# Attention scores and mixes made beside the second aggregation pass by TensorE products, with a scattered tail for sources of the last 14 node tiles

## The chip, the cores and the metric

The kernel runs on one NeuronCore of a Trainium2 chip. A core has five engines with queues of their own: TensorE (PE, with its weight loads shown as PEld), VectorE (DVE), ScalarE (ACT), GpSimd (POOL) and SyncE (SP). SP and ACT issue plain DMAs; POOL issues the indirect DMAs, which gather or scatter rows by indices that lie in on-chip memory (SBUF). PSUM is the small memory that PE writes. The time is the device time of one execution in microseconds (us), as a median of runs.

## The reference, cut to what matters

There are N = 12500 nodes of D = 256 features and 200000 edges sorted by their target `dst`. Two blocks follow each other: a graph convolution in two passes (each a sum over edges into the target node, then a product with a weight), and one attention block.

```python
h = relu(layernorm(x));  x = x + gcn(h)          # two passes over all 200000 edges
h = relu(layernorm(x))
xt = (h @ weight).reshape(n, 4, 64)              # 4 heads of 64
alpha_l = einsum('ehd,hd->eh', xt[src], attn_l)  # per edge, per head
alpha_r = einsum('ehd,hd->eh', xt[dst], attn_r)
alpha = softmax(leaky_relu(alpha_l + alpha_r, 0.01), axis=heads)
tmp = einsum('nh,nhd->nd', alpha[:n], xt[dst[:n]])   # only the FIRST n edges are used
out = x + tile(tmp, 4)
```

The attention block uses only the first n = 12500 edges, one per output row: row e of the output needs the scores of edge e. Since the edges are sorted by target, the targets of these edges are the first few hundred nodes (up to node 788 in the drawn inputs), while their sources lie anywhere among all nodes.

## The kernel before, in words

Nodes are handled in NT = 98 tiles of P = 128. Edges are handled in tiles of 128 too, J = 14 tiles to a chunk, NCH = 112 chunks. After a preparation of some 130 us come two passes over all edges, both made by `convolve` (L1153). For each edge tile, POOL gathers the 128 source rows from a table in DRAM (L1374, tile `fgot`), DVE makes one-hot matrices of the targets for a whole chunk (L1241, tile `fhot`), and PE multiplies the two and sums in PSUM (L1382, tile `facc`). `fgot` has four buffers of one chunk each in pass 2, so POOL can run ahead of PE by up to three whole chunks and the rest of one. A finished chunk is turned (`turn_sums`, L1202 to L1208) and added to a running transposed buffer (L1293). When all edges of a node tile w have been added, its finishing steps are queued.

The order of the work on every engine is written out by hand, in slots: one slot is one edge tile `t`. `at(t, step)` (L1167) puts a step down for a later slot, and `run(t)` (L1392) emits, after each tile's product, the steps that are due. In pass 2 the finishing steps of node tile w come from `finish2` (L1464), at offsets 6 to 28 slots: the products with the last two weights, the residual sum `fx` (stored to `kept_x`, L1495), the layernorm (L1497 to L1509), the transposes (L1514), and the product `fpx` with `fwg` (L1527). `fwg` holds the attention weight and, as eight more columns, that weight folded with `attn_r` and `attn_l`. So `fpx` gives, per node, its row xt, four right scores and four left scores. The left scores go to a DRAM table `table_l` (and to `table_e`, which leaves out the last three tiles), and for the first nine node tiles xt and the right scores go to `table_r`. Near the end of a pass the offsets are shortened to one slot each.

SP's queue holds, per node tile, the loads of the next tile's rows (`rb`, `fxb`, `self`) and the store of `kept_x`. An instruction that waits holds up all that stand behind it on its engine, and DMAs of one issuing engine follow each other.

After the second pass comes the attention's own stage, which we call the tail. The row of an edge's target, xt and right scores, is a product of a one-hot matrix (`hot_t`, L1572) and a gathered block of `table_r` (`rows`, L1577), copied out by ACT (`fends` to `fxg`, L1652 and L1654). For the first chunk this is done in pass 2 already. The left scores of an edge's source are gathered by POOL from `table_l`, one indirect DMA per tile of 128 edges (`fal`, L1662): 98 of them. DVE then adds, takes the softmax over the heads (L1669 to L1678), mixes the heads (L1685 to L1692) and adds the residual (`fres`, L1694), in 13 groups of G = 7 tiles and a last one split in two; SP loads `kept_x` (`fxr`, L1624) and stores the output (L1700, L1703). The first two groups are gathered from `table_e`, and what the last three tiles lack there is added by products (`lacks`, L1633).

Of the kernel before, what the change touches and what calls it, by code (L numbers as in the profile page):

```python
# [8 lines left out]
F32 = mybir.dt.float32  # L9
# [404 lines left out]
def fast_path(  # L414
# [62 lines left out]
    assert AC * J == NT and AC * CE <= E and XW < NT  # L477
    table_r = dram.tile([XW * P, DR], F32, name="table_r")
    table_l = dram.tile([NT * P, H], F32, name="table_l")

    LW = 3
    table_e = dram.tile([NT * P, H], F32, name="table_e")
# [18 lines left out]
    base_b = const.tile([P, NCH], F32, name="base_b")  # L501
    row_i = const.tile([P, AC], I32, name="row_i")
# [88 lines left out]
    with tc.tile_pool(name="fprep", bufs=1) as prep:  # L591
# [233 lines left out]
        with tc.tile_pool(name="fpsum", bufs=2, space=PSUM) as psum, \  # L825
# [227 lines left out]
            wide = prep.tile([NCH, P], F32, name="wide")  # L1053
            nc.vector.tensor_copy(wide, base.to_broadcast([NCH, P]))
# [7 lines left out]
            nc.tensor.matmul(fk[:, 2, :NCH], wide, ident[:NCH, :NCH], start=True, stop=True)  # L1062
# [7 lines left out]
            for f in after:  # L1070
                f()
            after = [raw_block(ends, m, psum.tile([P, 4 * P], F32, name="ft"), j0)
                     for j0 in (8, 12)]
            nc.vector.tensor_copy(base_b, fk[:, 2, :NCH])
            nc.vector.tensor_scalar(row_i, base_b[:, :AC], lane, float(XW * P - 1), op0=ALU.add,
                                    op1=ALU.min)
# [16 lines left out]
    def check_chunks(work, psum):  # L1093
# [20 lines left out]
        kept = work.tile([1, 1], F32, name="n_kept", bufs=1)  # L1114
        nc.vector.tensor_reduce(kept, pt[:1, 2, :NCH], AX.X, ALU.add)
        nc.vector.tensor_add(kept, kept, counted)
        nc.vector.tensor_scalar(bad_row, kept, -1.0, float(NCH + 1), op0=ALU.mult, op1=ALU.add)
# [12 lines left out]
    def load_late(pool):  # L1130

        nc.scalar.dma_start(roots, root_t)
        for t, w in ((wb, w2), (wo, w_post), (wg[:, :, :D], w_gat)):
            nc.scalar.dma_start(t, w.rearrange("(k p) n -> p k n", p=P))
        nc.scalar.dma_start(b2c, b2.rearrange("(k p) -> p k", p=P))
# [8 lines left out]
    def late_weights(pool, attn):  # L1144

        for i, ar in enumerate(attn):
            for k in range(KC):
                prod = pool.tile([P, H, C], F32, name="fprod", bufs=1)
                nc.vector.tensor_mul(prod.rearrange("p h c -> p (h c)"), wg[:, k, :D], ar)
                nc.vector.tensor_reduce(wg[:, k, D + i * H:D + (i + 1) * H], prod, AX.X,  # L1150
                                        ALU.add)

    def convolve(ep, table, stride, width, ahead, with_sum, psum, prepare, finish, lacking=False,  # L1153
                 raw=(), rows_p=None):
# [28 lines left out]
        def run(now=None):  # L1183

            while due:
# [3 lines left out]
                do(d)  # L1189

# [41 lines left out]
        const_p = psum.tile([P, P if with_sum else P + D], F32, name="iota_p", bufs=1)  # L1232
# [520 lines left out]
```

## Time and profile before

| what | value |
|---|---|
| median of 5 runs (lowest to highest) | 4148.24 us (4144.22 to 4149.51) |
| the profiled execution's own time | 4153.36 us |
| its span, first to last instruction | 4151.4 us |
| mean granted TensorE clock | 0.805 of full speed |
| busy: PE, PEld, DVE, ACT, POOL | 3083.6, 1955.9, 1139.4, 491.4, 3104.3 us |
| gathers of the passes (L1374) | 3056 with 947 ns each |
| gathers of the tail (L1662) | 98, 95.3 us busy in all |
| HBM traffic | 498.89 MB read, 53.21 MB written |

How to read it: "busy" counts only executing instructions, and an average over the whole span mixes the preparation, the two passes and the tail, which have different limits. Between two gathers POOL is always idle for 0.30 us with the cause "issue", that is, it waited for nothing that the profile shows; so a gather costs POOL 1.25 us and not 0.95.

### The profile page before, as it was taken

To read this page: it belongs to the slowest core of one execution; us is meant where nothing else is said; L and a number is where in the kernel's file an instruction comes from. 1 tells how busy PE (TensorE), PEld (TensorE's weight loads), DVE (VectorE), ACT (ScalarE), POOL (GpSimd) and SP (SyncE) were. 2 spreads that over 40 slices of the span, in tenths; PEclk is the share of its full clock that TensorE was granted. 3 is DMA by queue.
4 is the path that set the end of the run, shared out by engine and by line. 5 is a ranking of instruction groups with operands and counts; after the bars stand their busy time and mean duration, and the time that the engine had idled before them with its cause. 6 is when DMAs were issued, how large, how long until landed. Compare 5 with 4: busy or idle time off the path is not lost. (4 is left out here: it accounts for less than half of the span.)

```text
span 4151.4 us, 32267 instructions
## 1 busy us (share of the span) xinstructions
PE 3083.6 (74%) x10600; PEld 1955.9 (47%) x10600; DVE 1139.4 (27%) x2421; ACT 491.4 (12%) x1233; POOL 3104.3 (75%) x3299
## 2 busy tenths in 40 slices
PE   6687887877788877877587777776777777777774
PEld 5464444444444444443365545554555544544562
DVE  8532111111111111111232222222222222222238
ACT  5400000000000000000011111111111111111122
POOL 7677777777777777777777777777777777777766
PEclk8698778788877778788698888788878888888877
DMA  8644444444444444444544544554555445554556
GB/s 270 194 126 122 120 120 120 122 120 120 120 122 120 120 120 121 120 119 120 150 125 134 131 128 126 128 131 128 128 128 132 128 128 128 132 127 125 131 158 205
DMA packets 327420, 554.57 MB, mean 134 GB/s; under 512 B 96302, under 2 KB 224837, under 8 KB 327245
## 3 DMA queue, kind: packets, MB, share of 16 engines
q0 software_dynamic: 153520, 414.16, 37.8%
q1 hardware_dynamic: 127878, 121.99, 9.7%
q10 hardware_dynamic: 45846, 16.27, 1.6%
q8 instruction: 87, 1.43, 0.1%
q14 instruction: 89, 0.72, 0.1%
HBM read 498.89 MB, written 53.21 MB: 133 GB/s over the span
## 5 line engine op out<-in xcount | busy, mean ns | idle before, releaser
L1374 POOL DMA_INDIRECT fgot<-ftable,fsrc_t x3056 | 2892.5, 947 | 947.8 <-issue 880.2
L1382 PE MATMUL facc<-fgot,fhot 128*128 128x257 f32 (+1 forms) x6252 | 2335.2, 493 | 901.2 <-DMA fgot<-ftable,fsrc_t 859.5
L1382 PEld LDWEIGHTS facc<-fgot,fhot 128*128 128x128 f32 x6252 | 1252.1, 230 | 1824.4 <-DMA fgot<-ftable,fsrc_t 1402.8
L1293 DVE TENSOR_TENSOR buf<-buf,fturn 128x256 f32 x224 | 94.5, 422 | 1635.5 <-PE fturn L1206 1305.6
L1241 DVE TENSOR_TENSOR fhot<-iota_p,to_t 128x1792 f32<-128x1792 f32 x224 | 448.8, 2004 | 4.4 <-PE fpt L1267 4.4
L1479 DVE SCALAR_TENSOR_TENSOR fy<-rb,fb2c,fpz 128x128 f32<-128x128 f32 x194 | 58.8, 345 | 722.4 <-PE fpz L1472 721.4
L1276 ACT ACTIVATE fsums<-facc 128x257 f32<-128x257 f32 (+1 forms) x224 | 86.2, 385 | 1172.7 <-PE facc L1382 1158.3
L1493 DVE SCALAR_TENSOR_TENSOR fx<-fpo,fdinv,fxb 128x256 f32<-128x256 f32 x97 | 46.9, 484 | 496.1 <-PE fpo L1488 496.1
L1417 PE MATMUL fpo<-wf,buf 128*128 128x256 f32 x388 | 153.8, 540 | 0.3 <-DVE buf L1293 0.3
L1422 ACT ACTIVATE fo<-fpo,fdinv 128x256 f32<-128x256 f32 x97 | 46.0, 474 | 748.3 <-PE fpo L1418 746.5
L1417 PEld LDWEIGHTS fpo<-wf,buf 128*128 128x128 f32 x388 | 111.6, 288 | 28.0 <-DVE buf L1293 0.8
L1472 PE MATMUL fpz<-buf,fwb 128*128 128x128 f32 x776 | 116.5, 299 | 0.0
L1472 PEld LDWEIGHTS fpz<-buf,fwb 128*128 128x128 f32 x776 | 113.3, 221 | 2.1 <-DVE fy L1479 0.3
L1206 PE MATMUL fturn<-fident,self 128*128 128x128 f32 x396 | 83.7, 297 | 37.0 <-DMA to_all<-in_src_dram 24.1
L1488 PE MATMUL fpo<-fwo,fz 128*128 128x256 f32 x388 | 110.8, 410 | 0.1
L1662 POOL DMA_INDIRECT fal<-table_l,fsrc_t x84 | 81.5, 970 | 25.6 <-issue 23.2
L1206 PE MATMUL fturn<-fident,fsums 128*128 128x128 f32 x448 | 95.2, 298 | 0.5 <-ACT fsums L1276 0.5
L1652 PE MATMUL fends<-rows,hot_t 128*128 128x260 f32 x168 | 65.5, 548 | 35.9 <-ACT fxg L1654 35.2
L1518 ACT ACTIVATE ht<-fpt 128x256 f32<-128x256 f32 x97 | 37.2, 384 | 446.3 <-PE fpt L1514 446.3
L668 POOL DMA_INDIRECT fgot<-in_x_dram,raw_i x56 | 74.5, 1331 | 15.4 <-issue 15.1
L1206 PEld LDWEIGHTS fturn<-fident,fsums 128*128 128x128 f32 x448 | 69.7, 156 | 30.9 <-issue 7.6
L1418 PE MATMUL fpo<-bb,fins 2*128 2x256 f32 x194 | 83.0, 513 | 0.0
(267 smaller groups left out, 1720.2 us busy)
## 6 DMA issues: line engine op xcount, KB each, us to landing
fgot<-ftable,fsrc_t POOLq DMA_INDIRECT x3056
self<-ftable SPq DMA_DIRECT2D x99, 128.0 KB
self<-ftable SPq DMA_DIRECT2D x97, 130.0 KB
ftable<-fo ACTq DMA_DIRECT2D x98, 128.0 KB
kept_x<-fx SPq DMA_DIRECT2D x98, 128.0 KB
fxb<-in_x_dram SPq DMA_DIRECT2D x97, 128.0 KB
fxr<-kept_x SPq DMA_DIRECT2D x13, 896.0 KB
out_dram<-fres SPq DMA_DIRECT2D x13, 896.0 KB
```

Of the source, the lines that this page charges most:

```text
L668: nc.gpsimd.indirect_dma_start(out=raw[c][:, j, :D], out_offset=None, in_=x[:], in_offset=bass.IndirectOffsetOnAxis(ap=raw_i[:, k:k + 1], ...
L1206: nc.tensor.transpose(v["pt"][:, i * KC + k, :], rows[:, k * P:(k + 1) * P], ident)
L1241: nc.vector.tensor_tensor(h, iota_p[:, None, :].to_broadcast([P, n, P]), to[:, :, None].to_broadcast([P, n, P]), ALU.is_equal)
L1276: nc.scalar.activation(sb, acc, AF.Copy)
L1293: nc.vector.tensor_add(b, b, v["pt"][:, :KC, :])
L1374: nc.gpsimd.indirect_dma_start(out=got, out_offset=None, in_=table[:(NT - TW) * P, :] if some else table[:], in_offset=bass.IndirectOffset ...
L1382: nc.tensor.matmul(acc, hots[c][:, j, :], got[:, :width], start=(j == 0), stop=(j == nj[c] - 1 and not some))
L1417: nc.tensor.matmul(po, buf[:, k, :P], wf[:, k, :], start=(k == 0), stop=False)
L1418: nc.tensor.matmul(po, fs, bb, start=False, stop=True)
L1472: nc.tensor.matmul(pz[:, m, :], wb[:, k, m * P:(m + 1) * P], buf[:, k, :P], start=(k == 0), stop=(k == KC - 1))
L1488: nc.tensor.matmul(po, v["z"][:, m, :], wo[:, m, :], start=(m == 0), stop=(m == KC - 1))
L1662: nc.gpsimd.indirect_dma_start(out=al[:, i, :], out_offset=None, in_=(table_l if c else table_e)[:], in_offset=bass.IndirectOffsetOnAxis(a ...
```

## The change

The tail of before is taken out. Its work is put in small pieces into the free places of pass 2 (and a list is made in pass 1), and a short new tail treats the edges whose source lies in the last 14 node tiles (84 to 97), of which the drawn inputs have 1707 among the first 12500; the list has room for 2048.

- In pass 1, once 11 node tiles are finished, `list_late` makes, by products with one-hot matrices, a compact list of those "late" edges (KL = 16 columns of 128) with their place, their source and their target; it also stores to DRAM the low seven bits of the sources (`lo_rows`) and the targets relative to the first target of each tile (`rel_rows`).
- `convolve` gets a second queue, `behind`. `feed(t)` takes the next item from it when the item's condition holds and the place is free, and puts its parts into consecutive slots.
- In pass 2 the items are, in this order: load the target rows of each edge tile (98 loads from `table_r` at an address held in a register), the right scores (`alpha_r`, 14 groups of 7 tiles), the one-hots and target rows of the late edges (to DRAM), the left scores in five stages (`alpha_l`, after 18, 36, 54, 72 and 84 node tiles; each stage multiplies a one-hot of the low bits with the left scores of its node tiles, now kept in SBUF as `l_all`, and masks by the high bits), and with the fifth stage the softmax, the mix by products, the residual sum and the store (`group`).
- `table_l`, `table_e`, the 98 gathers of `fal`, the seven gathers of `rows`, the `hot_t`, `hot_l` and `lacks` work are gone.
- After pass 2, for the late edges: 16 gathers of `kept_x`, left scores by 16 products, softmax, mix and 16 indirect scatters of whole rows into the output.

```diff
+    STAGES = [(0, 18), (18, 36), (36, 54), (54, 72), (72, 84)]
+    LATE = STAGES[-1][1]
+    KL = 16
+    LIMITS = [LATE if k < 10 else LATE + G if k == 10 else NT for k in range(KL)]
...
+        def feed(t):
+            if behind and t >= free_at[0] and behind[0][0]():
+                _, space, parts = behind.pop(0)
+                for i, part in enumerate(parts):
+                    if part:
+                        at(t + i, lambda _, part=part: part())
+                free_at[0] = t + space
...
+            feed(t)
             run(t)
-        run()
+        if at_end:
+            at_end()
+        while due or behind:
+            t += 1
+            feed(t)
+            run(t)
...
         def r():
-            if w < NT - LW:
-                xa = work.tile([P, DA], F32, name="fxa")
-            else:
-                xa = lates[w]
-            nc.scalar.activation(xa[:, d0:], v["px"], AF.Copy)
-            nc.scalar.dma_start(table_l[w * P:(w + 1) * P, :], xa[:, DR:])
-            if w < NT - LW:
-                nc.scalar.dma_start(table_e[w * P:(w + 1) * P, :], xa[:, DR:])
             if w < XW:
-                nc.scalar.dma_start(table_r[w * P:(w + 1) * P, :], xa[:, :DR])
+                xa = work.tile([P, DR], F32, name="fxa", bufs=1)
+                nc.scalar.activation(xa, v["px"][:, :DR], AF.Copy)
+                nc.scalar.dma_start(table_r[w * P:(w + 1) * P, :], xa)
+            nc.scalar.activation(l_all[:, w, :], v["px"][:, DR - d0:], AF.Copy)
+            mark("w", w)
...
+        def row_of(rows, b, name, bufs):
+            r = ap.tile([P, HE], BF16, name=name, bufs=bufs)
+            nc.sync.dma_start(r, rows[b * G:(b + 1) * G, :].rearrange("t p -> (t p)")
+                              .partition_broadcast(P))
+            return r
+        def hot_of(row, col):
+            hot = new_hot()
+            nc.vector.scalar_tensor_tensor(hot, row, 0.0, banks[col].to_broadcast([P, HE]),
+                                           op0=ALU.subtract, op1=ALU.is_equal)
+            return hot
+        def ends_of_tile(t):
+            at = start_of(t, (XW * P - NB) * H)
+            nc.sync.dma_start(ends[:, t, :], by_head[bass.ds(at, P), :])
...
+        def alpha_l(s, b):
+            def load():
+                v["row"] = row_of(lo_rows, b, "lo_all", 1)
+            def equal():
+                v["h"] = hot_of(v["row"], "lane")
+            def product():
+                v["p"] = bank()[:, :G * nw * H].rearrange("p (t w h) -> p t w h", t=G, h=H)
+                for j in range(G):
+                    nc.tensor.matmul(v["p"][:, j, :, :], v["h"][:, j * P:(j + 1) * P],
+                                     l_all[:, w0:w1, :], start=True, stop=True)
+            def taken():
+                mask = ap.tile([P, G, 18], F32, name="mask", bufs=1)[:, :, :nw]
+                nc.vector.tensor_tensor(mask, ... ALU.is_equal)
+                nc.vector.tensor_tensor(v["p"], v["p"], ... ALU.mult)
+                nc.vector.tensor_reduce(some, v["p"].rearrange("p t w h -> p t h w"), AX.X, ALU.add)
+                nc.vector.tensor_add(al[:, t, :], al[:, t, :], some)
+            return [load, None, equal, product, taken]
+        def group(b):
+            def load():
+                load_lo()
+                v["rel"] = row_of(rel_rows, b, "rel_all", 2)
+                if whole:
+                    v["kept"] = load_kept(b * G, G)
...
+            return [load, None, equal, product, taken, lambda: v["soft"][0](),
+                    lambda: v["soft"][1](), turn, turned, over(0, 4), weigh(0, 4), over(4, G),
+                    weigh(4, G), mix, end]
...
+        for t in range(0, NT, G):
+            items.append((when("w", XW), G, [lambda t=t + i: ends_of_tile(t) for i in range(G)]))
+        for b in range(NG):
+            items.append((when("w", XW), 4, alpha_r(b)))
+        for b in range(KL // 4):
+            items.append((when("w", XW), 6, late_hots(b)))
+        for k in range(KL):
+            items.append((when("w", XW), 4, late_ends(k)))
+        for s in range(len(STAGES) - 1):
+            for b in range(NG):
+                items.append((when("w", STAGES[s][1]), 4, alpha_l(s, b)))
+        for b in range(NG):
+            items.append((when("w", LATE), 8, group(b)))
+        for t0, n in ((LATE, G), (LATE + G, 4), (LATE + G + 4, 3)):
+            items.append((when("x", t0 + n), 1, rest(t0, n)))
...
+    def tail_begins():
+        rows_x.close()
...
+        nc.sync.dma_start(sets["hot"], late_hot)
+        nc.sync.dma_start(sets["end"], late_end[:].rearrange("(k p) d -> p k d", p=P))
...
+        fetch_x(LATE + G)
...
+        for k in range(KL):
+            nc.tensor.matmul(z[k // 8][:, k % 8, :, :], sets["hot"][:, k * P:(k + 1) * P],
+                             l_all[:, LATE:, :], start=True, stop=True)
...
+        for n in [2, 2] + [4] * ((KL - 4) // 4):
+            nc.vector.tensor_mul(near, heads[:, k, :, :C], ...)
+            nc.vector.tensor_reduce(mix, near.rearrange("p k h c -> p k c h"), AX.X, ALU.add)
+            nc.vector.tensor_tensor(res, res, ... ALU.add)
+            for i in range(k0, k0 + n):
+                nc.gpsimd.indirect_dma_start(
+                    out=out[:], out_offset=bass.IndirectOffsetOnAxis(ap=late_i[:, 0, i:i + 1],
+                                                                     axis=0),
+                    in_=sets["x"][:, i, :], in_offset=None)
```

`load_kept` loads seven tiles of `kept_x` (896 KB) into one of two buffers, and `end` of a whole group adds the mix to it and stores it to the output from the same buffer. `late_ends` and `late_hots` each make 128 (or 4 times 128) one-hots, transpose them, and store their result to DRAM; `rest` adds the mixes of the last 14 tiles to `kept_x` and stores them.

In the order that is built, every scatter into the output waits for the landing of the scatter before it, since all write the same tensor; the loads of `tail_hot` and `tail_end` stand in SP's queue ahead of the last node tile's loads of `rb` and `fxb`; and the load of `lo_all` for group b + 2 stands in SP's queue behind the store of group b's output.

## The prediction

> **What bounds the kernel now.** I read the groups by cost first, then the sums by stretch for pass 2 and the tail, then the timeline at the seams.
>
> ```profile
> span 4151.4 us, 32267 instructions
> ...
> L1374 POOL DMA_INDIRECT fgot<-ftable,fsrc_t x3056 | 2892.5, 947 | 947.8 <-issue 880.2
> L1382 PE MATMUL facc<-fgot,fhot 128*128 128x257 f32 (+1 forms) x6252 | 2335.2, 493 | 901.2 <-DMA fgot<-ftable,fsrc_t 859.5
> ```
>
> POOL waits for nothing ("issue"); PE waits for the gathers. The passes last as long as POOL has gathers to issue, 0.947 + 0.30 = 1.25 us each.
>
> ```profile
> 2026.00:3986.00 1960.00, 1403.36 (x5349) 984.95 (x5348) 526.20 (x1103) 235.32 (x625) 1480.93 (x1564) 0.82 0.50 130
> 3991.00:4151.00 160.00, 89.48 (x300) 60.91 (x300) 113.86 (x223) 39.93 (x116) 97.59 (x101) 0.69 0.63 198
> ```
>
> Columns: stretch, length, busy PE, PEld, DVE, ACT, POOL with counts, granted clock, DMA share, GB/s. In pass 2 PE has 28% free, DVE 73%, the DMA engines half. The tail is 160 us long.
>
> ```profile
> 2026.75 0.94 POOL L1374 DMA_INDIRECT fgot<-ftable,src  x1 [2.15 <-DMA ftable<-fo]
> 2071.62 2.08 PE L1382 MATMUL facc<-fgot,fhot 128*128 128x256 f32 x4 [3.10 <-DVE fhot L1241]
> ...
> 3985.49 0.95 POOL L1374 DMA_INDIRECT fgot<-ftable,fsrc_t  x1 [0.30 <-issue]
> 3989.40 1.46 PE L1382 MATMUL facc<-fgot,fhot 128*128 128x256 f32 x6
> 4005.73 0.94 POOL L1662 DMA_INDIRECT fal<-table_e,fsrc_t  x1 [11.79 <-DMA table_l<-fxl]
> 4129.62 0.94 POOL L1662 DMA_INDIRECT fal<-table_l,fsrc_t  x1 [0.30 <-issue]
> 4144.73 0.70 SPq L1703 DMA_DIRECT2D out_dram<-fres  x1
> ```
>
> At pass 2's start PE begins 45 us after POOL's first gather and POOL never waits: PE may fall 45 us behind unseen. PE's last edge product ends at P = 3990.86. From there to the end are 160.5 us, of which 98 gathers of left scores take 98 x 1.25 = 122 us on POOL. That is what the change removes.
>
> **The change, part by part.**
>
> *POOL in pass 2.* Gone: one gather of `rows` (1.25 us) and the wide integer compares (L1572, L1595) at its start, beside which four gathers took 1.42, 1.46, 1.53 and 1.82 us instead of 0.95, that is 2.4 us. POOL paces, so -3.7 us. The new compares take an operand from PSUM, as `fhot` does, beside which gathers keep 0.95. If all 84 new one-hot operations of 896 columns cost POOL 0.5 us, it would be +42; I take 0, by `fhot`.
>
> *The list in pass 1.* 14 times three wide operations (about 1.0, 0.2 and 0.8 us by the columns of similar DVE rows) and some 60 small ones of 0.2 us are 40 us of DVE in 124 slots (155 us), where DVE is 18% busy, and 98 bf16 products on PE. Hidden behind POOL, 0; without that cover 40.
>
> *Target rows.* SP issues 98 loads, one per slot, each with a register load. The same on DVE leaves 0.36 us between L1499 and L1293; with 0.45 us of issue 0.8 us, under 1.25. 0; even at 1.8 us each SP would be 54 us late in mid-pass, which POOL's lead nearly covers.
>
> *Stages 0 to 3 and the late one-hots.* An item has 4 slots, 5 us. DVE: one-hot 1.09 (row L1685, 896 columns), wait for 14 product instructions, 2.1 us (`lacks`: 42 in 6.15 us), then 1.7 for mask product, sum and add, and 1.3 of its own pass work: up to 6.2. A stage of 14 falls at most 17 us behind, and the next comes 294 slots later. 0.
>
> *The fifth stage (`group`) decides.* It starts when node tile 83 is done: slot 1399 of 1563 (chunk 96 ends at slot 1357, then 13 and 28). Each of 14 groups has 8 slots, 10.0 us. In SP's queue the load `lo_all` of group b + 2 stands behind the 896 KB store of group b, which waits for DVE's `add_mix` of b. DVE, in order, can't do the one-hot of b + 2, nor what stands behind it (the second weights and the `add_mix` of b + 1, the next chunk's `fhot`), before that load has landed. From the end E of `add_mix`(b):
>
> - `lo_all` usable: 896 KB took 5.85 us from issue to use at one place and 7.67 at another.
>
> ```profile
> 2038.84 7.63 SPq L1567 DMA_DIRECT2D to_all<-in_dst_dram  x2
> 2044.69 1.42 DVE L1572 TENSOR_SCALAR hot_t<-to_all,base_b,lane 128x1792 f32<-128x1792 int32 x1 [14.35 <-DMA fgot<-ftable,src]
> ...
> 4005.05 2.87 SPq L1567 DMA_DIRECT2D to_all<-in_dst_dram  x3
> 4012.72 1.22 DVE L1572 TENSOR_SCALAR hot_t<-to_all,base_b,lane 128x1792 f32<-128x1792 int32 x1 [10.37 <-DMA to_all<-in_dst_dram]
> ```
>
>  With 224 KB more behind it: E + 7.5.
> - one-hot 1.09: 8.6; 14 product instructions 2.1: 10.7; an edge tile 0.5 and the mix's 14 instructions 2.1: 13.3 (DVE's softmax steps lie beside these); `add_mix` as L1694, 2.02: 15.3. Every other period node-tile work of DVE falls in between: 15.5.
>
> So 5.5 us are lost in each of 11 periods, 60; the last two groups wait once more, 5 above plan: PE is 65 us behind at slot 1506. POOL stops for some of it, but what counts is PE. 57 tiles are left. Catching up, PE needs per chunk 14 x 0.49 (six instructions, three tiles, in 1.46 us at 3989.40) + 0.875 x 3.05 (one node tile: 1.06 + 1.11 + 0.38 + 0.50 in the timeline at 3005 to 3012) + 0.8 = 10.3, or 0.74 per tile instead of 1.25: 29 us won back. With 4 us for the residual loads of `rest`: P comes 40 us late. Lower bound 0 (the load lands in time), upper bound 75 (a period of 18.8).
>
> *The new tail, from P.* SP loads 3.2 MB (`tail_hot`, `tail_end`), and the last tile's `rb` and `fxb` stand behind it. At 364 GB/s (the fullest 10 us of before, 4010 to 4020) 8.8 us, with seven gathers of `kept_x` between and the landing P + 14; before, the step that needs `rb` began at P + 6.9. So the last `fx` is at P + 17 (before: 4000.96, P + 10.1), its store landed at P + 20.7 (a 128 KB store to DRAM: 2023.27 to the POOL start that waits for it, 2026.75, 3.5 us), the last five gathers issued by P + 27. Left scores at P + 21.5, 32 product instructions 5, masks and sums 2.7, softmax 3 with a table load, first mix 2.1: first scatter at P + 34. Then 16 scatters, each waiting for the one before:
>
> ```profile
> 3007.73 0.94 POOL L1374 DMA_INDIRECT fgot<-ftable,fsrc_t  x1 [0.30 <-issue]
> 3010.47 0.70 PE L1382 MATMUL facc<-fgot,fhot 128*128 128x256 f32 x2 [0.50 <-DMA fgot<-ftable,fsrc_t]
> ```
>
> A gather of the same 128 KB is used 2.74 us after its start; with POOL's 0.30 that is 3.05, the lower end. The store above, with POOL's 0.95 in place of the issue of 0.33, gives 4.1, the upper end. I take 3.3, nearer the same kind of instruction: 53 us. P + 87, and 3 us to the end (before, 6 from the last issue to the end, 3.5 of it landing): P + 90. Kept low and high: 85 and 103.
>
> The Trainium skill, "DMA: Bandwidth & Descriptors", section "Anatomy of one DMA", speaks against a chain of such transfers: each costs about 2.0 us plus its bytes over 436 GB/s, mostly the wait for the write to be confirmed. By it a scatter is 2.3 us and sixteen are 37 us, an estimate 16 us under mine; the rows above say 3.05 and more.
>
> *Sum, against the profiled execution.* P = 3990.86 - 3.7 + 40 = 4027; + 90 = 4117 against a span of 4151.4: -34 us. The profiled execution (4153.36 us) is 5 us above the median of the runs; I take the difference over: 4148.24 - 34 = **4114 us**.
>
> **The rivals.**
>
> *The fifth stage keeps up.* If `lo_all` lands within 2.5 us of its issue, DVE needs about 7 us of new work and 2.7 of its own per 10, and P is not late: -3.7 - 70.5 = -74, **4074 us**. For it: half the DMA engines' time is free, and PE and DVE rest a lot. Against: the store ahead in the same queue, and a group moves 2.25 MB in 10 us, which with the 130 GB/s of the pass is 355 GB/s, about the fullest stretch seen (364).
>
> *Slower: PE runs cold in the fifth stage.* Its period becomes product and mix at half clock. `lacks` took 8.96 us instead of 6.15 for the same 42 instructions elsewhere in the tail. From a period of 18.8 us on, the loss (11 x 3.3 = 36 us more) eats the gain; at 20 us the time is **4163 us**. For it: in the tail of before the windows 4020 to 4030 and 4030 to 4040 were granted 0.50 with PE 7.90 and 10.00 us busy. Against: PE still has two edge tiles per gap to work on, and pass 2 as a whole was granted 0.82, no 100 us of it from 2100 on less than 0.78. "TensorE: Matmul & The Clock Gate", section "What's actually happening", of the Trainium skill says that the clock is 1.2 GHz until PE has been busy for about 3.4 us; by it the 4.2 us of products and mix would be near 8 and the period 19, at this rival's edge.
>
> *The change does not do its work:* if one of its checks on the data failed, the general path would run and double the time. The drawn inputs have 1707 late edges for 2048 places, at most 12 nodes in a tile for 32, and 69 in a column of 128 late edges for 128: 1%.
>
> **How the numbers follow.** Forecast (stage late by 15 to 60 us) 0.55, alone 4092 to 4137; keeping up 0.28; slower 0.13 with what else may cost; no change 0.03; general path 0.01. 0.2% (8 us) is what a measurement can tell here. Faster: 0.55 x 0.97 + 0.28 = 0.81, same 0.06, slower 0.13. The range goes from the second case with the cheap scatter (4074 - 4) to the slower one's beginning: 4070 to 4152.
>
> **What would show it.** In the changed profile: (1) POOL at 1.25 us per gather until about slot 1450, then waits for `facc`; (2) between two `add_mix` of whole groups 15.5 us, DVE idle before `hot_s` with the load of `lo_all` as cause; (3) PE's last `facc` at 4027, against 3987 if the stage keeps up; (4) `rb` of the last tile landing 14 us after it; (5) scatters 3.3 us apart, each waiting for the one before, the first 34 us after P. I am wrong if the stage's period is 10 or over 19, or if gathers slow down all through pass 2.

## The result, and the profile after

The changed kernel takes **4162.49 us** (median of 24 runs, 4150.32 to 4177.62), the kernel before 4150.69 (median of 47). The ratio is 1.0031, 95% interval 1.0025 to 1.0037: 0.3% slower, where 4114 us were forecast. The profiled execution has a span of 4159.7 us against 4151.4.

In nine of the runs below PE stopped for microseconds at a time through the whole program (the kernel before takes 4919 to 4925 us there), so these nine stand in a section of their own and are compared only with the kernel before of the same set.

The page of the changed kernel, first line and the two groups that were shown of before:

```profile
span 4159.7 us, 36108 instructions
...
L1397 POOL DMA_INDIRECT fgot<-ftable,fsrc_t x3056 | 2891.2, 946 | 999.7 <-issue 894.6
L1405 PE MATMUL facc<-fgot,fhot 128*128 128x257 f32 (+1 forms) x6252 | 2281.0, 483 | 708.9 <-DMA fgot<-ftable,fsrc_t 673.8
```

A gather still takes 0.946 us. But POOL's idle time ahead of the gathers has grown by 52 us (947.8 to 999.7), while the part in which it waits for nothing but issue has only grown by 14: something stops POOL now. The sums by stretch say where (columns as before: length, PE, PEld, DVE, ACT, POOL busy, granted clock, DMA share, GB/s): pass 2 up to the fifth stage, the fifth stage up to PE's last edge product, the tail.

```profile
2026.00:3776.00 1750.00, 1355.68 (x5819) 999.08 (x5819) 648.04 (x1332) 221.70 (x611) 1323.47 (x1401) 0.85 0.50 143
3776.00:4067.00 291.00, 249.95 (x1167) 210.02 (x1166) 147.54 (x319) 50.06 (x112) 153.47 (x162) 0.75 0.65 197
4067.00:4159.00 92.00, 18.59 (x80) 15.96 (x80) 26.16 (x49) 6.79 (x18) 31.37 (x32) 0.54 0.31 95
```

Up to 3776 POOL is busy 76%, its steady pace of one gather in 1.25 us: the stages 0 to 3, the list and the target rows are free, as forecast. In the fifth stage POOL falls to 53%, and PE is busy 86% at a clock of 0.75. The tail is 92 us long instead of 160.

At the seams, from the timeline: POOL's first long stop, PE's last edge product, the use of the last `rb`, and the first two and the last scatter.

```profile
3927.88 0.94 POOL L1397 DMA_INDIRECT fgot<-ftable,fsrc_t  x1 [13.04 <-PE facc L1405]
...
4065.34 1.46 PE L1405 MATMUL facc<-fgot,fhot 128*128 128x256 f32 x6
...
4080.91 0.60 DVE L1749 SCALAR_TENSOR_TENSOR fy<-rb,fb2c,facc 128x128 f32<-128x128 f32 x2 [7.11 <-DMA rb<-roots]
...
4102.62 1.01 POOL L2169 DMA_INDIRECT out_dram<-tail_x,late_i  x1 [8.70 <-DVE tail_x L2166]
4105.34 0.98 POOL L2169 DMA_INDIRECT out_dram<-tail_x,late_i  x1 [1.72 <-DMA out_dram<-tail_x,late_i]
...
4146.29 0.97 POOL L2169 DMA_INDIRECT out_dram<-tail_x,late_i  x1 [2.41 <-DMA out_dram<-tail_x,late_i]
```

So P, the end of the last edge product, is 4066.8 instead of 3990.9: 75.9 us later, where 36 were forecast. From P to the end are 92.9 us instead of 160.5: 67.6 us won, where 70.5 were forecast. 75.9 - 67.6 = 8.3 us is the difference of the spans. Of the error of 42.7 us in the span (4117 forecast), 39.8 lie in P, that is, in the fifth stage and what follows it up to P; 2.9 lie in the tail.

One of its periods, from the addition of one whole group to that of the next, in the timeline:

```profile
3821.25 2.02 DVE L1979 TENSOR_TENSOR fxr<-fxr,behind 128x1792 f32<-128x1792 f32 x1 [2.06 <-PE behind L2033]
...
3823.30 0.39 SPq L1833 DMA_DIRECT2D out_dram<-fxr  x1
...
3823.78 0.52 SPq L1854 DMA_DIRECT2D lo_all<-lo_rows  x1
...
3827.29 0.75 DVE L2025 SCALAR_TENSOR_TENSOR weights<-rel_all,node_q,behind 128x512 f32<-128x512 bf16 x1 [3.46 <-PE behind L2018]
...
3829.76 1.09 DVE L1860 SCALAR_TENSOR_TENSOR hot_s<-lo_all,iota_p 128x896 f32<-128x896 bf16 x1 [1.72 <-DMA lo_all<-lo_rows]
...
3830.99 2.97 PE L1961 MATMUL behind<-l_all,hot_s 128*128 128x48 f32 x14 [1.82 <-DVE hot_s L1860]
...
3833.76 2.04 PE L1405 MATMUL facc<-fgot,fhot 128*128 128x256 f32 x4
...
3835.59 3.09 PE L2033 MATMUL behind<-ends_all,weights 128*128 128x64 f32 x14
...
3838.72 2.02 DVE L1979 TENSOR_TENSOR fxr<-fxr,behind 128x1792 f32<-128x1792 f32 x1 [2.63 <-PE behind L2033]
```

The order is the one foreseen: the load of `lo_all` is issued behind the store, the one-hot waits for it, products, mix and addition follow. The period is 17.47 us (2.02 addition, 6.49 to the one-hot, 1.09 one-hot, 0.14, products 2.97, 1.63 to the mix, mix 3.09, 0.04). Over the eleven periods of whole groups it is (3998.20 - 3801.26) / 11 = 17.9 us, not 15.5. Two things differ from the plan. The load makes DVE idle for only 1.72 us of its 6.49, since up to 3828.0 DVE waits for another chain: the softmax of the group before, PE's turn, ACT's copy, PE's spread over the nodes, the first `weights`. And PE is slow: 14 products take 2.97 us and 14 mixing products 3.09, with 2.1 each in the plan, and the four instructions of two edge tiles 2.04, where the same four take 1.03 at 4044.88, at a full clock.

### The profile page after: what moved, and what is told of

Same layout as the page of the kernel before. It is cut to its first block, busy times and chain, and to the rows that moved or that the text cites. A ratio compares the mean times of both kernels' runs of the same rounds, so it can differ in the third digit from the quotient of the medians.

```text
span 4159.7 us, 36108 instructions
## 1 busy us (share of the span) xinstructions
PE 3201.7 (77%) x12112; PEld 2129.7 (51%) x12112; DVE 1363.2 (33%) x2895; ACT 494.4 (12%) x1233; POOL 3031.6 (73%) x3226
## 5 line engine op out<-in xcount | busy, mean ns | idle before, releaser
L1397 POOL DMA_INDIRECT fgot<-ftable,fsrc_t x3056 | 2891.2, 946 | 999.7 <-issue 894.6
L1405 PE MATMUL facc<-fgot,fhot 128*128 128x257 f32 (+1 forms) x6252 | 2281.0, 483 | 708.9 <-DMA fgot<-ftable,fsrc_t 673.8
L1961 PE MATMUL behind<-l_all,hot_s 128*128 128x72 f32 (+1 forms) x980 | 149.1, 314 | 72.5 <-DVE hot_s L1860 46.6
L1749 DVE SCALAR_TENSOR_TENSOR fy<-rb,fb2c,fX 128x128 f32<-128x128 f32 x194 | 58.7, 344 | 424.5 <-PE fX L1742 422.8
L1961 PEld LDWEIGHTS behind<-l_all,hot_s 128*128 128x128 f32 x980 | 144.4, 230 | 86.7 <-issue 84.6
L1763 DVE SCALAR_TENSOR_TENSOR fx<-fX,fdinv,fxb 128x256 f32<-128x256 f32 x97 | 46.8, 482 | 381.0 <-PE fX L1758 381.0
L1742 PE MATMUL fX<-buf,fwb 128*128 128x128 f32 x776 | 130.8, 324 | 0.0
L1742 PEld LDWEIGHTS fX<-buf,fwb 128*128 128x128 f32 x776 | 126.9, 245 | 2.8 <-issue 0.9
L1758 PE MATMUL fX<-fwo,fz 128*128 128x256 f32 x388 | 112.2, 414 | 3.3 <-ACT fz L1752 2.9
L1860 DVE SCALAR_TENSOR_TENSOR hot_s<-lo_all,iota_p 128x896 f32<-128x896 bf16 x70 | 75.7, 1082 | 47.3 <-DMA lo_all<-lo_rows 47.2
L1969 DVE TENSOR_TENSOR behind<-behind,mask 128x504 f32<-128x504 f32 (+1 forms) x70 | 46.0, 657 | 121.3 <-PE behind L1961 119.9
```

Source lines behind the costliest of these rows:

```text
L1397: nc.gpsimd.indirect_dma_start(out=got, out_offset=None, in_=table[:(NT - TW) * P, :] if some else table[:], in_offset=bass.IndirectOffset ...
L1405: nc.tensor.matmul(acc, hots[c][:, j, :], got[:, :width], start=(j == 0), stop=(j == nj[c] - 1 and not some))
L1742: nc.tensor.matmul(pz[:, m, :], wb[:, k, m * P:(m + 1) * P], buf[:, k, :P], start=(k == 0), stop=(k == KC - 1))
L1749: nc.vector.scalar_tensor_tensor(y[:, m, :], v["root"], b2c[:, m:m + 1], v["pz"][:, m, :], op0=ALU.mult, op1=ALU.add)
L1758: nc.tensor.matmul(po, v["z"][:, m, :], wo[:, m, :], start=(m == 0), stop=(m == KC - 1))
L1860: nc.vector.scalar_tensor_tensor(hot, row, 0.0, banks[col].to_broadcast([P, HE]), op0=ALU.subtract, op1=ALU.is_equal)
```

## The experiments

Theory 1 was the prediction's: the load behind the store sets the period. Theory 2: PE does, by its work at the granted clock. In the table P is the end of the last edge product, the period is the distance of the first and the twelfth addition of a whole group over 11, the clock is the mean over 3800 to 4000, all from the profiled execution; the ratio is to the kernel before of the same set.

| kernel | period | clock | P | time (median) | ratio, 95% interval |
|---|---|---|---|---|---|
| changed | 17.9 | 0.70 | 4066.8 | 4162.5 | 1.0031, 1.0025 to 1.0037 |
| e1b_store_act | 16.1 | 0.76 | 4042.0 | 4143.6 | 0.9989, 0.9974 to 1.0004 |
| e2b_few_products | 15.8 | 0.69 | 4043.6 | 4140.3 | 0.9976, 0.9966 to 0.9986 |
| e3b_no_group | none | 0.85 | 3995.4 | 4090.7 | 0.9858, 0.9838 to 0.9877 |
| e5_tail_act | 16.0 | 0.76 | 4042.1 | 4136.6 | 0.9972, 0.9961 to 0.9984 |
| e6_early_lo | 15.3 | 0.80 | 4036.9 | 4132.1 | 0.9956, 0.9939 to 0.9973 |
| e7_early_few | 14.4 | 0.71 | 4032.5 | 4128.9 | 0.9949, 0.9929 to 0.9969 |
| e8_early_tail | 15.5 | 0.78 | 4038.2 | 4123.2 | 0.9935, 0.9918 to 0.9952 |
| e9_early_act | 15.6 | 0.77 | 4048.0 | 4127.2 | 0.9941, 0.9924 to 0.9958 |
| e11c_fill | 13.1 | 0.96 | 4015.1 | 4105.6 | 0.9898, 0.9881 to 0.9914 |

### The price of the stage: e3b_no_group

```diff
-        for b in range(NG):
-            items.append((when("w", LATE), 8, group(b)))
-        for t0, n in ((LATE, G), (LATE + G, 4), (LATE + G + 4, 3)):
-            items.append((when("x", t0 + n), 1, rest(t0, n)))
```

> Same kernel as e3_no_group (the fifth stage and its additions and stores left out). Both theories: last edge product at 3987, POOL never stopped, a tail of 93 us, 4080 us. A last product later than 3990 would put a part of the loss into the earlier stages.

P is 3995.4 and the tail 93.6 us. POOL is never stopped where the fifth stage stood. The 8 us above 3987 were lost at the start of pass 2, in one wait that no kernel with the groups has (waits of POOL, 2000 to 3990; columns: sum, times, longest):

```profile
POOL fgot L1397 <- ACT pick L2126: 14.3, 1, 14.3
```

The other run of the same kernel (e3_no_group, below) has this wait too, with 38.0 us, so it comes with leaving the groups out, and why is not known. The fifth stage therefore costs at least 71 us of P and 72 us of time (4162.5 - 4090.7), and up to 86 us of P if this wait is taken off; nothing else of the change is visibly late.

### The load: e1b_store_act

```diff
     def store_out(t0, n, res):
...
-            nc.sync.dma_start(out[n0:n0 + k * P, :]...
+            nc.scalar.dma_start(out[n0:n0 + k * P, :]...
```

> Same kernel as e1_store_act (the store of a finished group from ACT's queue), on a chip where the kernel before takes 4150 us. Theory 1 (the load sets the period): last edge product at 4007, time near 4103 us. Theory 2 (PE's work at its granted clock sets it): last edge product 4047 to 4066, time 4143 to 4162 us.

P is 25 us earlier, the time 19 us less: less than half of what theory 1 asks, at the end of theory 2's range by the time and 5 us below it by P. The store was not the only thing in front of the load. In one period of this kernel the load stands behind the store of a node tile's `kept_x`, and DVE waits 5.88 us for it. Ahead of such stores SP waits for DVE six times between 3790 and 4000, 46.4 us in all.

```profile
3878.92 0.32 SPq L1765 DMA_DIRECT2D kept_x<-fx  x1
...
3882.09 0.48 SPq L1854 DMA_DIRECT2D lo_all<-lo_rows  x1
...
3888.79 1.09 DVE L1860 SCALAR_TENSOR_TENSOR hot_s<-lo_all,iota_p 128x896 f32<-128x896 bf16 x1 [5.88 <-DMA lo_all<-lo_rows]
```

### The products: e2b_few_products

```diff
-                for j in range(G):
+                for j in range(G if s < len(STAGES) - 1 else 1):
                     nc.tensor.matmul(v["p"][:, j, :, :], v["h"][:, j * P:(j + 1) * P], ...
...
-                for j in range(G):
+                for j in range(1 if whole else G):
                     nc.tensor.matmul(v["p"][:, j, :], v["w"][:, j * P:(j + 1) * P], ...
```

(The masks and the additions read other data for the missing six sevenths.)

> Same kernel as e2_few_products (one of seven score products in the fifth stage, one of seven mixing products in its whole groups; the rest of the products is left out and other data stands in). Theory 1: the period stays at 14 us or more, last edge product about 4030, time about 4123. Theory 2: the period falls to 10 to 12 us, last edge product 3990 to 4010, time 4083 to 4103.

P is 4043.6, the time 4140.3: theory 2, which asked for a period of 10 to 12 us, fails here, and P and time are 14 and 17 us later than theory 1 has them. With 24 of 28 product instructions gone from each period it shrinks by 2.1 us only. DVE waits for the load as long as before (19.7 us in ten waits from 3790 to 4000, 19.1 in the changed kernel), as theory 1 has it, and PE, busy less, is granted no more: the sums of 3850 to 3900, and one one-hot of the timeline.

```profile
3850.00:3900.00 50.00, 37.02 (x137) 29.10 (x137) 28.98 (x65) 10.86 (x22) 38.12 (x40) 0.66 0.84 258
```

```profile
3856.96 1.09 DVE L1860 SCALAR_TENSOR_TENSOR hot_s<-lo_all,iota_p 128x896 f32<-128x896 bf16 x1 [3.70 <-DMA lo_all<-lo_rows]
```

### Both: e6_early_lo and e7_early_few

Theory 3: the load and PE's work stand in series. `lo_all` is now issued five slots earlier, ahead of the store.

```diff
+            def ahead():
+                product()
+                if b + 1 < NG:
+                    lo_of[b + 1]()
...
-            return [load, None, equal, product, taken, ...
+            return [load, None, equal, ahead, taken, ...
```

> The load of lo_all for a group is issued five slots earlier (right behind the score products of the group before), so that in SP's queue it stands ahead of the store of the group before; the store stays in SP's queue. Theory 3 (the load and PE's work stand in series in each period): DVE no longer waits for lo_all, the period falls from 17.9 to 12.6 to 14.5 us (the periods of e1b_store_act in which DVE did not wait), last edge product 4015 to 4030, time 4110 to 4125 us. Theory 2 (PE's work at its granted clock alone): no better than e1b_store_act, last edge product 4040 or later, time 4140 or more.

> The early load of e6_early_lo together with the missing products of e2b_few_products (one of seven score products in the fifth stage and one of seven mixing products in its whole groups are made, other data stands in). Theory 3: neither of the two parts is left, the period falls to 10 to 11.5 us and the last edge product comes at 3995 to 4010 (3995 without the stage), time 4090 to 4105. If a third thing holds the period (DVE's order, the bytes of 2.25 MB per group), it stays at 13 us or more and the last product at 4020 or later.

In e6 DVE has no wait for `lo_all` left, and P comes 30 us earlier, the time is 30 us less, both between the ranges of theory 3 (4015 to 4030, 4110 to 4125) and of theory 2 (4040 and 4140 or more), and the period of 15.3 is above theory 3's 14.5. In e7, with the products gone too, the period is still 14.4: the answer reserved for a third thing. Its nature shows in e6, in two periods that follow each other. Instructions of PE in the timeline:

```profile
3897.71 1.76 PE L1961 MATMUL behind<-l_all,hot_s 128*128 128x48 f32 x14
...
3906.15 0.37 PE L2016 MATMUL behind<-fident,al_all 128*28 128x128 f32 x1 [3.32 <-DVE sc L1775]
...
3916.04 3.06 PE L1961 MATMUL behind<-l_all,hot_s 128*128 128x48 f32 x14
```

and the sums around them:

```profile
3890.00:3900.00 10.00, 9.06 (x57) 7.42 (x57) 5.53 (x12) 2.03 (x4) 7.55 (x8) 1.00 0.88 266
3900.00:3910.00 10.00, 6.68 (x33) 5.31 (x32) 7.54 (x18) 2.83 (x6) 7.56 (x8) 0.76 0.99 326
3910.00:3920.00 10.00, 10.00 (x39) 8.64 (x38) 3.34 (x6) 0.39 (x1) 7.56 (x8) 0.50 0.84 261
```

Before the turn PE pauses for 3.32 us, until DVE has made the addition of the group before and the softmax. Behind the pause the same 14 products take 3.06 us instead of 1.76; the granted clock is 0.50 over ten microseconds in which PE is busy without a gap, and it stays there for 20 us in all:

```profile
3905.20:3925.50 20.30, 19.35 (x72) 16.66 (x73) 9.59 (x21) 1.78 (x5) 15.42 (x17) 0.50 0.74 233
```

That period lasts 20.5 us (additions at 3903.4 and 3923.9), the one before 14.2, the one behind 13.0. And e7, with less work and more pauses, is at 0.71 where e6 is at 0.80. Theory 4: pauses of PE cost it the clock for most of the next period. Theory 5: a chain of handovers between DVE, ACT and PE is as long as the period, whatever the clock.

### The pause filled: e11c_fill

Ahead of each turn, where PE pauses, it makes two products that nothing reads.

```diff
             def turn():
                 v["p"] = bank()
+                for _ in range(2):
+                    nc.tensor.matmul(v["p"][:, P:2 * P + 2 * P], ident,
+                                     ends[:, :6, :C], start=True, stop=True)
                 nc.tensor.transpose(v["p"][:G * H, :P], ...
```

> Same kernel as e11_fill (two products that nothing reads ahead of each turn, on e8_early_tail, which took 4123 us with a last edge product at 4037.5 and a mean period of 15.5). Theory 4 (PE's pauses cost its clock): mean period 14 us or less in spite of 22 to 45 us of added work, last product earlier than 4037.5, time below 4123 us. Theory 5 or PE's bare amount of work: periods 0.5 to 1.6 us longer, last product 4045 to 4060, time 4130 to 4145 us.

What theory 4 forecast comes true, and what theory 5 forecast does not: with 1.45 us more work in each group the time falls from 4123.2 (e8_early_tail, the same kernel without the filling, on another chip) to **4105.6 us**, P from 4038.2 to 4015.1, the period from 15.5 to 13.05. Against the kernel before of its own set each, 0.9935 becomes 0.9898, and the intervals do not meet. The sums from the first to the twelfth addition, of the changed kernel, of e8 and of e11c:

```profile
3801.26:3998.20 196.94, 171.40 (x776) 144.48 (x776) 104.71 (x222) 34.50 (x71) 119.22 (x127) 0.70 0.73 222
3801.36:3971.70 170.34, 156.45 (x776) 131.25 (x776) 104.19 (x221) 34.38 (x71) 116.72 (x124) 0.76 0.81 255
3805.74:3949.26 143.52, 137.63 (x826) 113.17 (x826) 103.70 (x221) 34.21 (x70) 108.49 (x116) 0.97 0.93 294
```

The first two make the same 776 instructions on PE; e11c makes 50 more in less busy time, at a clock of 0.97. PE's waits at the turn fall from 12.3 us in e8 (nine, the longest 3.3) to 5.3 (five, the longest 1.9). What is left above 10 us is mostly work: PE is busy 96% of the stretch, 12.5 us per period, 1.45 of them the filling.

How pauses and clock go together shows in the traces of e6 and e8 over the same stretch: the granted clock falls to 0.5 eleven times. Six of these falls begin within 4.5 us of the start of a pause of 2.2 to 3.3 us, and the clock stays down for 14 to 21 us. The other five have no pause of over 1.2 us ahead of them, and last 7 to 10 us. One pause of 2.2 us (e6, at 3835.8) brings no fall. In e11c no pause of over 2 us is left, and there is one fall, of 7 us. So the long falls go with the pauses; what brings the short ones is not known. The filling also gives PE more to do, and whether taking the pause away without it does as much was not measured on a chip like this (e10, below).

e11c is the fastest version found, 1.0% under the kernel before and 1.4% under the changed one.

### The tail: e5_tail_act, e8_early_tail, e9_early_act

e5 is e1b and e8 is e6, both with the two large loads on ACT's queue:

```diff
-        nc.sync.dma_start(sets["hot"], late_hot)
-        nc.sync.dma_start(sets["end"], late_end[:]...
+        nc.scalar.dma_start(sets["hot"], late_hot)
+        nc.scalar.dma_start(sets["end"], late_end[:]...
```

> As e1b_store_act, and the two large loads of the tail (tail_hot, tail_end, 3.2 MB) are issued from ACT's queue, so that the last tile's rb and fxb do not stand behind them in SP's. If queue order delays rb (it is used 14 us after the last edge product in the changed kernel, 7 us in the kernel before), it is used at 7 to 9 us, the first scatter moves from 36 to about 30 us behind the last product, and the time is 5 to 7 us below that of e1b_store_act. If the bytes delay it (3.2 MB take 9 us whatever the queue), rb is used at 12 to 14 us and the time is within 2 us of e1b_store_act.

> e6_early_lo, and tail_hot and tail_end loaded from ACT's queue. In e5_tail_act this brought rb 6 us earlier, but there the last copies of l_all stood behind a store in ACT's queue for 6.6 us; here that store is in SP's. The first scatter comes 29 to 31 us behind the last edge product instead of 36, and the time is 5 to 7 us below that of e6_early_lo: 4103 to 4120 us by theory 3. If the loads' bytes set the step, no difference.

In e5 the last `rb` is used 8.3 us behind P (4042.1) instead of 14.1, so it was the queue's order and not the bytes that held it. But the first scatter still came 35.6 us behind P, as the last copies of `l_all` wait on ACT behind a store whose addition waits for its rows:

```profile
4050.40 0.60 DVE L1749 SCALAR_TENSOR_TENSOR fy<-rb,fb2c,facc 128x128 f32<-128x128 f32 x2 [0.82 <-ACT fz L1752]
...
4064.37 0.17 ACT L1805 ACTIVATE l_all<-fY 128x4 f32<-128x4 f32 x1 [7.41 <-DVE fxr L1979]
```

In e8, with that store on SP, the first scatter is issued at 4066.1, 28 us behind P, and from P to the end are 84.8 us instead of 93.1 in e6. The time is 9 us below e6's, though the intervals of the two ratios overlap.

e9 is e8 with the stores of whole groups on ACT's queue (`nc.scalar if t0 < LATE else nc.sync`):

> e8_early_tail, and the stores of whole groups from ACT's queue (those of the rest stay in SP's). If SP's order still holds back loads behind the store (rel_all, kept_x, rb, fxb), the period falls by another 1 to 2 us and the time by 10 to 20 us against e8_early_tail. If not, ACT's wait for the additions costs as much as it frees, and the two are within 5 us.

The period is the same (15.6), the time 4 us more, within its interval: with the load early, the store's queue makes no difference that shows. (Its P of 4048.0 comes from a pass 2 that ran 5 us behind e8's from its start, and a first addition 8 us later.)

### Runs in which PE stopped through the whole program

> The 896 KB store of a finished group is issued from ACT's queue instead of SP's, so that the load of lo_all for the group after next no longer stands behind it. Theory 1 (the prediction's: the load sets the period): of the 17.9 us between two additions of whole groups 5 to 6 go, in 11 periods 60 us; PE's last edge product comes at about 4007 instead of 4066.8, and the time is near 4103 us. Theory 2 (PE sets it: in the fifth stage it is busy 87% of the time at a granted clock of 0.7, and the load is covered by the chain of softmax, turn and weights of the group before): only DVE's idle time before the one-hots, 20 us in the whole stage, can go. Last edge product at 4047 to 4066, time 4143 to 4162 us.

> In the fifth stage's twelve whole groups one of the seven score products is made, and one of the seven mixing products; in all fourteen groups one score product. DVE works on as many elements as before (other data stands in for the missing products), so scores and rows are not those of the reference. Loads and stores are unchanged. Theory 1 (the load): 1.2 to 2 us of 17.9 go with each set of products as they stand in the chain behind the load, the load's 6.5 us stay: DVE waits more for lo_all, and the period stays at 14 us or more; last edge product about 4030. Theory 2 (PE): PE loses 5 us of its 15.5 busy us per period, stays warm, and the period falls to 10 to 12 us: last edge product 3990 to 4010.

> The fifth stage (the groups) and the additions of the rest are left out, with their loads and the stores of whole groups: rows with an early source are not written. It prices the stage. Both theories expect that POOL is never stopped and PE's last edge product comes at 3987 (that of before less 3 us), 80 us earlier than in the changed kernel, and that the tail of 93 us stays: 4080 us. If pass 2 loses time elsewhere, in the earlier stages or at its start, the last product comes later than 3990.

> The groups start 11 slots apart (13.75 us) instead of 8 (10 us); nothing else. If PE's sum of work sets the end (theory 2), it is the same sum, and the last edge product stays within 10 us of 4066.8: time 4150 to 4172 us. If a chain of 17.9 us per group sets the period, whatever PE has to do beside it (a latency, theory 1's kind), the edge tiles are done in its gaps and few are left after it: last edge product about 4035, time about 4130 us.

e4's edit is the number of slots of a group, 8 to 11. For the two that follow, e10's edit puts an empty slot ahead of `end` in the list of a group's steps (`mix, None, end`), on top of e8, and e11 is e11c's kernel; e10b and e11b repeat them, e10c repeats e10.

> e8_early_tail, and in each group the addition (2.02 us on DVE) is written one slot later, so that on DVE the second half of the next group's softmax stands ahead of it and PE's turn no longer waits for the addition. Theory 4 (PE is the bound once the load is early, and its pauses of 2 to 3 us at the turn halve its granted clock for the next period: 13.4 us where it stays warm, 20.5 where it does not): the pauses at the turn go, the long periods with them, the mean period falls from 15.5 to 13 us, last edge product 4010 to 4020, time 4095 to 4108 us. Theory 5 (a chain of handovers between DVE, ACT and PE sets the period, whatever the clock): at most the 2 us of the addition go from the chain, and only in the periods with a pause: period 14.5 to 15, last product 4028 to 4035, time 4113 to 4121.

> e8_early_tail, and ahead of the turn in each group PE makes two products of 384 columns that nothing reads (1.6 us at full clock, 3.2 at half), where it otherwise pauses; 14 groups, 22 to 45 us of more work. Theory 4 (the pause costs its clock): pauses of 2 us are filled, the long periods of 20 us become rare, mean period 14 us or less in spite of the added work, last product earlier than 4037.5, time below 4123 us. Theory 5 or PE's bare amount of work: every period grows by 0.5 to 1.6 us, last product 4045 to 4060, time 4130 to 4145 us.

> Same kernel as e10_add_later, on a chip where the kernel before takes 4150 us. Theory 4 (PE's pauses at the turn cost its clock): mean period 13 us instead of 15.5, last edge product 4010 to 4020, time 4095 to 4108 us. Theory 5 (a chain of handovers): period 14.5 to 15, last product 4028 to 4035, time 4113 to 4121.

> Same kernel as e11_fill. Theory 4: mean period 14 us or less in spite of 22 to 45 us of added work, last product earlier than 4037.5, time below 4123 us. Theory 5 or PE's bare amount of work: periods 0.5 to 1.6 us longer, last product 4045 to 4060, time 4130 to 4145 us.

> Same kernel as e10_add_later (on e8_early_tail, the addition one slot later, so that PE's turn does not wait for it). Filling the pauses gave a mean period of 13.05 us with 1.45 us of useless products in it, at a full clock from 3890 on, last edge product 4014.4, time 4105.6. If the pauses are gone without the filling, the period is 11.6 to 13 us, last product 4000 to 4015, time 4088 to 4106 us. If pauses of another cause stay (PE waits for the softmax itself, or for the addition at the next product that takes its bank), the clock falls again: period 14 to 15.5, last product 4025 to 4037, time 4110 to 4123.

Against the kernel before of the same set (4918.5 to 4925.0 us): e1 1.0483 (1.0433 to 1.0532), e2 1.0364, e3 1.0221 (1.0179 to 1.0263), e4 1.0501 (1.0457 to 1.0545); e10 1.0424, 1.0431 and 1.0398 (1.0344 to 1.0503, 1.0382 to 1.0481, 1.0321 to 1.0476); e11 1.0446 and 1.0410 (1.0362 to 1.0529, 1.0363 to 1.0457). How it looks there, in the timeline of e1: a product of PE that is shown as done at 2200.65, while ACT, which copies it out, starts ten microseconds later.

```profile
2199.96 0.69 PE L1447 MATMUL fpo<-bb,fins 2*128 2x256 f32 x2
...
2210.80 0.47 ACT L1451 ACTIVATE fo<-fpo,fdinv 128x256 f32<-128x256 f32 x1 [10.92 <-remote]
```

From 200 us on PE's instructions show 105 gaps of over 5 us in this run, 1.07 ms together; in the changed kernel's trace above there are four. POOL's gathers wait 623 us for PE's `facc` over the whole program, against 87 in the changed kernel's trace. So PE holds the gathers up there, and work that the change gives to PE costs time: without the fifth stage (e3) 101 us more than before although 68 us of tail are gone, with it (e1) 220 us more. The questions of e4 and e10 for a chip whose PE does not stop, whether groups further apart help and whether taking the pause away does as much as filling it, stay open: no run of them fell outside this condition.

## Why the prediction was wrong, point by point

- **The size of the gain** was right to 3 us, in part by luck: the tail from P is 92.9 us, forecast 90. The last `rb` was used 14.1 us behind P (forecast 14, its landing), and e5 shows that the place in SP's queue was the reason. The first scatter came at P + 35.8 (34). The scatters are (4146.29 - 4102.62) / 15 = 2.9 us apart (3.3; bounds 3.05 and 4.1), under the lower bound, since a scatter lands 2.4 us behind its issue where 2.74 were taken from a gather's use. The Trainium skill, "DMA: Bandwidth & Descriptors", section "Anatomy of one DMA", gave 2.3 us as an estimate for one: that agrees with the landing of 2.4, and POOL's waiting and issue make 2.9 of it. The 5.8 us that the 15 distances gave back were lost behind the last scatter (below): 13.4 us from its issue to the end, where 6.3 were forecast.
- **POOL in pass 2** was right in sign: the 2800th of its 3056 gathers comes 8.9 us earlier than before (3656.4 and 3665.4), forecast 3.7. The list, the target rows and the stages 0 to 3 cost nothing that shows.
- **The fifth stage** was the step that failed: "15.3: every other period node-tile work of DVE falls in between: 15.5", measured 17.9. Over 11 periods these are 26 of the 39.8 us by which P is off. The load was over-sized (7.5 from the addition's end to the one-hot, measured 6.49; of its two rows the one with 5.85 us ends a wait that the profile puts down to a gather and not to that load) and most of it covered by the chain of softmax, turn, spread and weights, which the prediction had left "beside these". The terms of PE were under-sized: products 2.1 (2.97), edge tile and mix 2.6 (1.63 and 3.09). Their durations were the faster of two rows, 6.15 us for 42 instructions of `lacks`; the slower, 8.96, or 3.0 for 14, is what the stage showed.
- **The catching up** behind the stage failed too, and makes the other 14 us. From the end of edge tile 1506 to P the kernel before takes 73.1 us and the changed one 61.7 (4005.1 to 4066.8): 11 us won back, where 29 less 4 were forecast. The sum has no term for the last two groups, whose products, spreads and mixes still take 20.6 us of PE's instructions in that stretch.
- **The rival "PE runs cold in the fifth stage"** named what happened, products and mix at about half clock, and got 0.13. That its number fits (4163 us, measured 4162) is luck: it belongs to a period of 20 us, and the mean period was 17.9, in a row of 14 to 21, below the 18.8 that it asked for; the catching up made the difference. It was dismissed because PE "still has two edge tiles per gap to work on, and pass 2 as a whole was granted 0.82". The clock was 0.67 from 3800 to 3900 and 0.72 from 3900 to 4000, with PE busy 87% of the time. DVE's softmax and addition and the load make PE pause about once in each period (13 waits for DVE from 3800 to 4000, 24.8 us). That less work alone hardly helps is shown by e2b and e7, that filling the pauses does by e11c.
- **"The stage keeps up"** (0.28) asked for a load that lands in time. e6 gave it that, and the period was still 15.3. The prediction never added up PE's own work: in e11c, at a clock of 0.97, it is 11.1 us of a period (12.5 less 1.45), already more than the 10 us of its slots.
- The signs (1) to (5): POOL stopped, but at 3914 and not at slot 1450, which is about 3840; DVE's wait with the load as cause is there, at 0.5 to 5.4 us; P was off by 40 us; (4) and (5) as above.

## What to carry to other kernels

Where work is moved beside other work, add up each engine's work in the stretch that covers it, at the clock that a stretch with pauses is granted, not at the mean: an engine that is "28% free" in the mean was over-full in the stage that mattered. When PE takes its turns with DVE through in-order queues, look for the waits of 2 to 5 us in front of its products: removing the load's and filling those at the turn took 30 and 18 us, leaving out six sevenths of the products 22 and 3 (the 3 are within the spread of the runs). In front of a load, look at every queue-mate that waits for a computation, not only the one nearest to it.

## What was not expected of the hardware

- A pause of 3.32 us went with a granted clock of 0.50 for 20 us (3905.2 to 3925.5 in e6), though PE was busy 19.35 of the 20.30 us. The Trainium skill, "TensorE: Matmul & The Clock Gate", section "What's actually happening", has the clock come back after some 3.4 us of activity. By that, as an estimate, a period would lose 1.7 us (3.4 us at half clock); measured were 6 to 7.5 (20.5 against 14.2 and 13.0). The measurement decides here.
- Useless products made the kernel faster by 15 to 18 us (0.9935 to 0.9898 of the kernel before; 4123.2 to 4105.6 us).
- The end of the program is longer behind a scatter. The trace's last instructions of POOL, behind the last scatter:

```
before: 4133.47 INC_SWDGE_SEM 1215 ns, 4134.72 DRAIN 4242 ns, end of the span 4151.4
after:  4149.99 INC_SWDGE_SEM 1868 ns, 4151.89 DRAIN 6937 ns, end of the span 4159.7
```

  In the kernel before they lie beside the last tiles' work; here nothing covers them, and from the last issue to the end are 13.4 us (before: 6.7, from the last store's issue at 4144.73).
- One chip was in a condition where PE stops for over 1 ms in all in one set of runs (e10, e11) and not in another (e6 to e9). Versions that take 0.999 and 0.990 of the kernel before without it (e1b, e11c) take 1.04 to 1.05 of it there (e1, e11).
